# Gated attention block on one core: the last chunk's x loaded at once and bo\*gate added ahead, the denominators' test in one matmul behind the last y, routing in four stages, and the third last tile's matmuls split two, one and one

## The chip, the cores and the metric

The kernel runs on one core of a Trainium2 chip. The metric is the device time of one execution in microseconds (us). An interval or a ratio is always against the kernel before on the same chip.

## What is computed

The input x is 2 batches of 1024 tokens with 512 features, all in float32. Two branches read the same layernorm of x, and their product is added to x:

```python
xn = layernorm(x)
# attention, 32 heads of 16 features, causal
q, k, v = (xn @ W.T + b for W, b in ((Wq, bq), (Wk, bk), (Wv, bv)))
att = softmax(where(causal, q @ k.T / sqrt(16), -inf))
s = (att @ v) @ Wo.T + bo
# gate: a base projection and 8 experts of rank 16, of which the best two are used
probs = softmax(xn @ W_gate.T)
top_p, top_i = top_k(probs, 2)
route_w = one-hot(top_i) weighted by top_p / sum(top_p)
hw = einsum('bnd,erd->bner', xn, A) * route_w
g = silu(xn @ W_base.T + b_base + einsum('bner,eor->bno', hw, B))
out = x + s * g
```

## The kernel before

**Chunks, units and steps.** Each batch is two chunks of 512 tokens, (b, c), and each chunk four tiles of 128 tokens. A unit (b, oc, c) is the attention of eight heads (oc is one of four groups of 128 features) for one chunk's queries. The units are cut into a plan of 144 steps. A step's scores are sixteen or eight or more matmuls `s` (L913, transposed: keys on partitions), an Exp on ScalarE into `pt` (L922), a causal mask on VectorE where the step has a diagonal block (`masked`, L941), and matmuls `av` with the values (L957), where a column of ones beside the values gives the denominators of the softmax.

**Program order.** The program is written out by hand, with no scheduler behind it. Each step issues the scores of step n, the values of step n - 1, the masks of step n, and then `fill(n)`. Each engine takes its instructions in this order. A step's score tiles use all the PSUM that scores have, so the next `s` waits for `pt` of the step before; `av` waits for the masks.

**Filler tasks.** `fill` gives TensorE other work, so many matmuls that the rest of the work is spread evenly over the remaining steps. The tasks are generators, sorted by a due step: `qk_task` (pq, pk), `v_task` (pv), `route_task` (ph: the experts' first projection and the routing logits), `gate_task` (pb, and then g, sg and g\*sg), `out_task` (po, the output projection). A task yields its cost in TensorE time (`MM`) after each block of 128 rows of a contraction, which the profile shows as eight matmuls, or `WAIT` where it may go on in the next step at the earliest. Tasks without a TensorE cost (layernorm, routing, the test) are stepped at the end of `fill`, behind the posts of finished units in `later`.

**Routing.** `routed_task` (L409) takes the logits of a chunk: maximum, difference (L427), Exp on ScalarE (L428), then the sum, reciprocal and product of a softmax, the top two with ties to the lower index (`top`), their normalization, the product `hw` with the experts' first projection and a transpose `hsq` (L457, L464), a DMA to DRAM, and back as `hwT` one step later. It is cut in two stages by one `WAIT`. `gate_task` may start three steps after it ended.

**Posts of a unit.** When a unit ends, VectorE copies its two av tiles to oT and avs (L978, L980). A few steps later the denominators, spread over partitions by way of DRAM, are inverted on VectorE (rc, L543), avs is halved on GpSimd (L547) and merged on VectorE (L548: merge), and the inverse is brought back by DMA into avs and multiplied in (rb, L556 and L557).

**Last chunk.** The last unit's steps go tile by tile: its av is copied to avs per tile (L975), turned (`pt_o`, L571), divided on VectorE (L579, L580: olast), turned again (`pt_y`, ScalarE copy L617) and put through po. Tiles 0 and 1 are `whole_task`, with three VectorE operations per tile: po + bo, times g, plus x. Tile 2 (the title's third last tile) is a `whole_task` with `hold`, which runs from the last step's fill on, with its last two operations on GpSimd (L633, L634). Tile 3 is `most_task` (three of four blocks of po, ahead: its y, times g, plus x go into base) and `rest_task` (the last block). Each tile loads its own x (xr, L87). The last `fill` gives tile 2 `3 * MM`, three of its four blocks; the fourth follows the second `pt_o`.

**Test.** The kernel divides without the maximum of a softmax; all denominators must lie in a range, else a general kernel behind a branch computes everything again. `test_task` tests those of the units before the last (`first_fine`). In `rest_task`, `all_in_range` tests the last unit's (L676, L677), takes the minimum over columns (L685), multiplies the two (L686), counts partitions with one matmul `pn` (L688) and writes the count to `sound` (L689). All engines read `sound` at the end and branch.

## Time and profile before

| | |
|---|---|
| median of 3 runs | 635.23 us (635.17 to 635.51) |
| the profiled execution's own time | 635.22 us |
| its span | 632.30 us, so 2.92 outside the span |
| granted TensorE clock | 0.995 |
| TensorE busy | 619.9 us, 98% of the span |
| ScalarE, VectorE, GpSimd busy | 47%, 45%, 16% |
| pt, Exp on ScalarE (L922) | 288 of 1.02 us |
| mask on VectorE (L941) | 166 of 0.61 us |
| avs halved on GpSimd (L547) | 15 of 1.70 us |
| g\*sg on GpSimd in one place (L514, 577.38) | 1.27 us |

In lines of the timeline the first number is the start in microseconds from the start of the span and the second is the time; `x8` is the number of instructions in the group. In brackets stands the idle time of the engine ahead of the group and what ended it. A step of the plan is seen on TensorE as one group of s, one of av and the filler.

### The profile page before, as it was taken

What the parts mean: (1) busy time and instruction counts of PE and PEld (TensorE: products, weight loads), DVE (VectorE), ACT (ScalarE), POOL (GpSimd) and SP (SyncE); (2) the same over time, 40 slices, a digit from 0 to 9 for tenths busy, and PEclk for the clock granted to TensorE, in tenths of its full rate; (3) what the DMA queues carried; (4) which work ended last, traced back from release to release, by engine and by line L of the source; (5) the groups of instructions that cost most, each with busy time, mean ns of one, the idle gap of its engine ahead of it and who ended that gap; (6) DMA issues with size and microseconds to landing.
All of it is one profiled execution on the core that took longest, in us unless ns stands there. A gap on an engine that the chain in (4) does not pass through costs nothing.

```text
span 632.3 us, 15592 instructions
## 1 busy us (share of the span) xinstructions
PE 619.9 (98%) x6911; PEld 232.5 (37%) x6911; DVE 283.8 (45%) x584; ACT 298.0 (47%) x336; POOL 104.1 (16%) x128
## 2 busy tenths in 40 slices
PE   8999999999999999999999999999999999999993
PEld 8335322322334333332333322342233343245651
DVE  4454722322593627640545522326245636143543
ACT  2425344555555556554434544254445555535550
POOL 2101000010122003320351103300013200242301
PEclk9999999999999999999999999999999999999998
DMA  9903000030013040220110001200000001121012
GB/s 270 277 37 104 24 18 2 2 71 1 2 49 96 1 101 4 73 87 1 56 64 6 5 20 44 76 4 20 18 4 3 4 6 53 35 69 51 7 36 72
DMA packets 29515, 29.61 MB, mean 47 GB/s; under 512 B 6920, under 2 KB 19728, under 8 KB 29440
## 3 DMA queue, kind: packets, MB, share of 16 engines
q1 hardware_dynamic: 29424, 28.53, 15.2%
q8 instruction: 56, 0.92, 0.6%
q14 instruction: 19, 0.16, 0.1%
q10 hardware_dynamic: 16, 0.00, 0.0%
HBM read 19.65 MB, written 8.88 MB: 45 GB/s over the span
## 4 chain that ended last, share of the span: by engine, by line
PE 93%; DVE 4%; issue 1%; POOL 1%; ACT 1%; POOLq 0%; DVEq 0%
PE s L913 24%; PE av L957 22%; PE pb L197 10%; PE po L197 8%; PE pq L197 8%; PE pv L197 8%; PE pk L197 8%; PE ph L197 2%; PE warm L149 1%; PE pq_first L306 1%; ACT pt L922 0%; PE pk_first L306 0%; POOL rstd L215 0%; PE pt_x L295 0%; DVE ok L677 0%
## 5 line engine op out<-in xcount | busy, mean ns | idle before, releaser
L922 ACT ACTIVATE pt<-s 128x1024 f32<-128x1024 f32 x288 | 279.0, 1020 | 263.7 <-PE s L913 263.6
L913 PE MATMUL s<-qT,kT 32*128 32x512 f32 (+3 forms) x1824 | 168.9, 464 | 0.3 <-ACT pt L922 0.2
L941 DVE TENSOR_TENSOR pt<-pt,causal 128x256 f32<-128x256 f32 (+1 forms) x166 | 99.2, 612 | 143.0 <-ACT pt L922 143.0
L957 PE MATMUL av<-pt,v 128*32 128x512 f32 (+3 forms) x1824 | 155.7, 443 | 0.3 <-DVE oT L978 0.2
L913 PEld LDWEIGHTS s<-qT,kT 32*128 32x128 f32 x1824 | 74.1, 184 | 119.8 <-ACT pt L922 79.7
L957 PEld LDWEIGHTS av<-pt,v 128*32 128x32 f32 x1824 | 43.6, 109 | 90.3 <-issue 68.2
L197 PE MATMUL pb<-wb_sb,xnT 128*32 128x512 f32 x512 | 61.9, 592 | 0.0
L197 PE MATMUL po<-wo_sb,oT 128*32 128x512 f32 x512 | 60.3, 593 | 0.4 <-ACT oT L617 0.4
L197 PE MATMUL pv<-wv_sb,xnT 128*32 128x512 f32 x512 | 60.0, 592 | 0.0
L197 PE MATMUL pq<-xnT,wq_sb 128*32 128x512 f32 x480 | 57.6, 592 | 0.0
L197 PE MATMUL pk<-xnT,wk_sb 128*32 128x512 f32 x480 | 56.8, 592 | 0.0
L513 POOL TENSOR_SCALAR sg<-sg 128x512 f32<-128x512 f32 x16 | 10.8, 672 | 259.8 <-ACT sg L512 259.8
L363 DVE TENSOR_SCALAR qT<-pq,b_sb,half 128x512 f32<-128x512 f32 x30 | 22.9, 805 | 49.4 <-PE pq L197 49.4
L547 POOL TENSOR_SCALAR avs<-avs,half 128x512 f32<-128x512 f32 x15 | 25.5, 1701 | 109.9 <-DMA den<-avs 85.6
L609 POOL TENSOR_TENSOR y<-y,g 128x512 f32<-128x512 f32 x12 | 15.3, 1274 | 90.8 <-DVE y L608 90.8
L197 PEld LDWEIGHTS pv<-wv_sb,xnT 128*32 128x32 f32 x512 | 16.8, 110 | 33.1 <-issue 32.4
L401 DVE TENSOR_TENSOR v<-pv,bv_sb 128x512 f32<-128x512 f32 x16 | 11.0, 690 | 39.7 <-PE pv L197 39.7
L197 PEld LDWEIGHTS pb<-wb_sb,xnT 128*32 128x32 f32 x512 | 16.7, 110 | 30.6 <-issue 29.9
L197 PEld LDWEIGHTS po<-wo_sb,oT 128*32 128x32 f32 x512 | 16.3, 110 | 31.5 <-issue 29.9
L197 PEld LDWEIGHTS pk<-xnT,wk_sb 128*32 128x32 f32 x480 | 15.5, 110 | 32.9 <-issue 32.6
L197 PEld LDWEIGHTS pq<-xnT,wq_sb 128*32 128x32 f32 x480 | 15.9, 110 | 30.7 <-issue 30.2
L512 ACT ACTIVATE sg<-g 128x512 f32<-128x512 f32 x16 | 10.1, 630 | 27.4 <-DVE g L509 20.3
(99 smaller groups left out, 318.9 us busy)
## 6 DMA issues: line engine op xcount, KB each, us to landing
x<-in_x_dram SPq DMA_DIRECT2D x16, 256.0 KB
xr<-in_x_dram SPq DMA_DIRECT2D x16, 256.0 KB
out_dram<-y SPq DMA_DIRECT2D x16, 256.0 KB
scr<-sq SPq DMA_DIRECT2D x6, 512.0 KB
xnT<-scr SPq DMA_DIRECT2D x24, 128.0 KB
wq_sb<-in_wq_dram SPq DMA_DIRECT2D x4, 256.0 KB
wk_sb<-in_wk_dram SPq DMA_DIRECT2D x4, 256.0 KB
wv_sb<-in_wv_dram SPq DMA_DIRECT2D x1, 1024.0 KB
```

The lines of the kernel that those rows point to most:

```text
L149: nc.tensor.matmul(warm[:, n % 4 * P : n % 4 * P + P], lhsT=ident, rhs=ident, start=True, stop=True)
L197: nc.tensor.matmul(o[j : j + 32], lhsT=lhsT[:, j : j + 32] if len(lhsT.shape) == 2 else lhsT[:, j // 32], rhs=rhs, start=start, stop=stop,)
L363: nc.vector.tensor_scalar(qT[:, par], pq, bq_sb[:, oc : oc + 1], half[:, par : par + 1], ALU.add, ALU.mult)
L401: nc.vector.tensor_add(vh[:, :, 0:HD], pv.rearrange("p (h r) -> p h r", h=H), bv_sb.rearrange("p (h r) -> p h r", h=H),)
L512: nc.scalar.activation(sg, gt, AF.Tanh, scale=0.5)
L513: nc.gpsimd.tensor_scalar(sg, sg, 0.5, 0.5, ALU.mult, ALU.add)
L547: nc.gpsimd.tensor_scalar(avs, avs, half[:, 1:2], None, ALU.mult)
L609: nc.gpsimd.tensor_tensor(y, y, gs.pop((b, i)), ALU.mult)
L913: nc.tensor.matmul(ss[s // 2][:, s % 2, col : col + w], lhsT=kT[rows, kt % TT * P : kt % TT * P + P], rhs=qTs[b, oc, c][rows, par, q0 : q0 ...
L922: nc.scalar.activation(pt[:, 2 * pair : 2 * pair + 2], ss[pair], AF.Exp, scale=0.25)
L941: nc.vector.tensor_tensor(d, d, mask, ALU.mult)
L957: nc.tensor.matmul(avs_now[par][32 * s : 32 * s + 32, q0 : q0 + w], lhsT=vs[b, kt][:, h * VS - HD * par : h * VS - HD * par + HP], rhs=pt[ ...
```

## The change

There are four parts.

1. The x of the last chunk comes in one DMA into the chunk tile (`bases_task`, due nine steps before the end) instead of four. `whole_task` forms bo\*g and adds it to x on GpSimd ahead of its po, so that `finish_tile` has two operations on VectorE: po times g, plus base.
2. `last_in_range` writes the test of the last unit's denominators as 32 columns of a tile `fine`, whose first column is the earlier test. One matmul with ones sums all 33 columns over partitions, behind the last po; VectorE reduces and copies the sum to `sound` behind the last y. The branch compares with 33 x 128.
3. The routing drops the softmax's division (it cancels in the normalization of the top two) and is cut in four stages: to the difference; Exp and the first `top`; the rest up to the weights; hw, hsq and the DMA.
4. The last `fill` gives two blocks of tile 2's po; a third is issued behind the last av, and the fourth where it was, behind the second `pt_o`.

```diff
+NF = 1 + 4 * 2 * 4
...
-    with tc.If(n < P, preferred_fallthrough_block=False):
+    with tc.If(n < P * NF, preferred_fallthrough_block=False):
...
         nc.vector.tensor_tensor(pr, lg, over(mx), ALU.subtract)
+        yield WAIT
         nc.scalar.activation(pr, pr, AF.Exp)
-        z = each("z")
-        nc.vector.tensor_reduce(z, pr, AX.X, ALU.add)
-        nc.vector.reciprocal(z, z)
-        nc.vector.tensor_tensor(pr, pr, over(z), ALU.mult)
...
         nc.vector.tensor_tensor(r1, r1, over(m1), ALU.mult)
+        yield WAIT
         hw = sb.tile([P, TT, ER], F32, tag="hw", bufs=1, name="hw")
...
+    def bases_task(b, c):
+
+        xt = chunk_tile(b, c)
+        nc.sync.dma_start(
+            out=xt, in_=x[b, c * C : (c + 1) * C].rearrange("(t p) d -> p t d", p=P)
+        )
+        for t in range(TT):
+            bases[t] = xt[:, t]
+        yield 0.0
+
+    def finish_tile(b, c, t, po):
+        i = c * TT + t
+        y = sb.tile([P, D], F32, tag="tmp", name="y")
+        nc.vector.tensor_tensor(y, po, gs.pop((b, i)), ALU.mult)
+        nc.vector.tensor_tensor(y, y, bases[t], ALU.add)
+        nc.sync.dma_start(out=out[b, i * P : (i + 1) * P, :], in_=y)
+
     def whole_task(b, c, t, hold=0):
...
-        while not turned or normalized(b, c) < KC - 1 or now[0] < hold:
+        while not turned or normalized(b, c) < KC - 1:
             yield WAIT
-        xt = load_x(b, i)
+        y, g = sb.tile([P, D], F32, tag="tmp", name="y"), gs[b, c * TT + t]
+        nc.gpsimd.tensor_tensor(y, bo_sb, g, ALU.mult)
+        nc.gpsimd.tensor_tensor(bases[t], bases[t], y, ALU.add)
+        while now[0] < hold:
+            yield WAIT
         po = mm_tile("po")
         for _ in project_out(po, b, c, t, 0, KC):
             yield MM
-        y = sb.tile([P, D], F32, tag="tmp", name="y")
-        nc.vector.tensor_add(y, po, bo_sb)
-        eng = nc.gpsimd if hold else nc.vector
-        eng.tensor_tensor(y, y, gs.pop((b, i)), ALU.mult)
-        eng.tensor_tensor(y, y, xt, ALU.add)
-        nc.sync.dma_start(out=out[b, i * P : (i + 1) * P, :], in_=y)
+        finish_tile(b, c, t, po)
         yield MM
...
     def rest_task(b, c, t):
...
+        last_in_range()
         yield lambda: turn_last(b, c, t, turned), TR
...
-        all_in_range()
-        y = sb.tile([P, D], F32, tag="tmp", name="y")
-        nc.vector.tensor_tensor(y, po, gs.pop((b, i)), ALU.mult)
-        nc.vector.tensor_tensor(y, y, bases[i], ALU.add)
-        nc.sync.dma_start(out=out[b, i * P : (i + 1) * P, :], in_=y)
+        pn = mm_tile("pn")[0:1, 0:NF]
+        nc.tensor.matmul(pn, lhsT=ones, rhs=fine, start=True, stop=True)
+        finish_tile(b, c, t, po)
+        count = small.tile([1, 1], F32, tag="count", bufs=1, name="count")
+        nc.vector.tensor_reduce(count, pn, AX.X, ALU.add)
+        nc.vector.tensor_copy(sound, count)
         yield MM
...
+    def last_in_range():
+        in_range(
+            fine[:, 1:NF], rc_last.rearrange("p a t s -> p (a t s)"), 1.0 / Z_HIGH, 1.0 / Z_LOW
+        )
...
+                Task(len(plan) - 9, bases_task(b, c), 0.0, after=before, takes={"x": 1})
...
         if n == len(plan) - 1:
-            even = 3 * MM
+            even = 2 * MM
...
     values(last, pts.pop(last))
+    third = next(x for x in tasks if x.begun)
+    third.step()
     turn_late()
```

## The prediction

> **What bounds the kernel now.** I read first the busy shares and the chain that ended last on the page.

> ```profile
> PE 619.9 (98%) x6911; PEld 232.5 (37%) x6911; DVE 283.8 (45%) x584; ACT 298.0 (47%) x336; POOL 104.1 (16%) x128
> PE 93%; DVE 4%; issue 1%; POOL 1%; ACT 1%; POOLq 0%; DVEq 0%
> ```

> TensorE's matmuls are the time. The changed program gives TensorE the same matmuls, but for the small one of the test, so only its stalls and the tail can move. A modelled busy time hides stalls, so the second view is the timeline of TensorE, where a step of the plan lasts from its first s to the next. With sixteen filler matmuls beside 4096 columns each of s and av, undisturbed steps last 3.78 to 3.81 us.

> ```profile
> 253.92 1.15 PE L913 MATMUL s<-qT,kT 32*128 32x256 f32 x16
> 257.71 1.14 PE L913 MATMUL s<-qT,kT 32*128 32x512 f32 x8
> 262.25 1.57 PE L913 MATMUL s<-qT,kT 32*128 32x512 f32 x8
> 435.55 2.05 PE L913 MATMUL s<-qT,kT 32*128 32x384 f32 x16 [0.20 <-ACT pt L922]
> 440.24 1.14 PE L913 MATMUL s<-qT,kT 32*128 32x512 f32 x8
> ```

> 253.92 to 257.71 is a whole step; 435.55 to 440.24 is 4.69, a stall of 0.89; 257.71 to 262.25 is 4.54, one of 0.76. Third, the timelines of the other engines say what each stall waited for.

> ```profile
> 434.13 0.19 DVE L427 TENSOR_TENSOR pr<-hl,mx 128x32 f32<-128x32 f32 x1
> ...
> 434.36 0.23 ACT L428 ACTIVATE pr<-pr 128x32 f32<-128x32 f32 x1 [3.46 <-DVE pr L427]
> ...
> 439.33 0.69 DVE L457 TENSOR_TENSOR hw<-hl,key 128x512 f32<-128x512 f32 x1
> ```

> The routing's Exp stands on ScalarE ahead of the next pt, whose s was done at 432.6, and waits for VectorE; then a row of small VectorE operations, with hw and hsq (0.71, from 440.06) at its end, stands ahead of masks that an av needs.

> **Routing in four stages.** Three small operations go (0.22 us each by their starts, 434.62 to 435.28). The Exp moves to the step after pr, so that ScalarE never waits, and hw and hsq (1.40 us) to a step of their own. The TensorE steps around the four routings exceed the whole step by: chunk (0,0) 0.69 and 0.31; (0,1) 0.32; (1,0) 0.26, 0.89 and 0.67; (1,1) 0.33. I take all of these as removed, 3.47, less 0.1 in (1,1), where the stage of eleven small operations (11 x 0.22 = 2.4) starts after kT at about 528.8 and so ends near 531.2, close ahead of masks that av needs by 532.2. Gain 3.4; bounds 1.0 (only what the Exp's wait and three operations cost) to 3.5. Step 124's stall of 0.85 stays: step 123 has no filler in either order, and its s waits for pt.

> **What the stages push.** hwT comes two steps later. In chunks (0,0) and (1,0) the order on TensorE is unchanged. In (1,1) po work is put ahead, and the gates land in steps without a merge beyond the one of before. In (0,1) the planner puts pv first, and g of tiles 5 and 7 finish in the same fills as rc and merge (steps 57 and 62), ahead of them on VectorE, and their sg and g*sg ahead of avs on GpSimd. One place of before has this very order:

> ```profile
> 575.19 0.68 DVE L509 TENSOR_TENSOR g<-pb,bb_sb 128x512 f32<-128x512 f32 x1
> 580.24 0.75 DVE L548 SCALAR_TENSOR_TENSOR oT<-oT,half,avs 128x512 f32<-128x512 f32 x1 [4.10 <-POOL avs L547]
> ...
> 576.68 0.62 POOL L513 TENSOR_SCALAR sg<-sg 128x512 f32<-128x512 f32 x1 [6.44 <-ACT sg L512]
> 577.38 1.27 POOL L514 TENSOR_TENSOR g<-g,sg 128x512 f32<-128x512 f32 x1
> 578.64 1.56 POOL L547 TENSOR_SCALAR avs<-avs,half 128x512 f32<-128x512 f32 x1
> ```

> Merge starts 5.05 us after g. There it costs nothing, since the next step has no masks; behind merge at step 57 stand four normalizations and the masks that av(58) waits for:

> ```profile
> 255.71 0.75 DVE L548 SCALAR_TENSOR_TENSOR oT<-oT,half,avs 128x512 f32<-128x512 f32 x1 [1.28 <-POOL avs L547]
> 256.38 1.91 DVE L222 TENSOR_SCALAR x<-x,mv,rstd 128x512 f32<-128x512 f32 x4
> 258.21 1.28 DVE L941 TENSOR_TENSOR pt<-pt,causal 128x512 f32<-128x512 f32 x2
> ```

> From merge's start to the masks' end is 3.78 us. g can start at 254.09, so merge at 259.14 instead of 255.71: av(58) and the next s come 3.43 later, of which 0.43 is won back, since g(6) no longer puts its sg ahead of pt in the step behind (its stall of before). Net 3.0. At step 62 g starts near 274.15, merge near 279.2, and the masks end about 280.4 to 280.7; av(63) began at 278.90. Cost 1.5. Sum 4.5; bounds 0 (the gates finish otherwise than their order says) and 5.0.

> **x and bo*gate early.** Four loads of x become one DMA of 1 MB at step 133. SP issues it behind back<-rc (576.16) and ahead of avs<-back, which waits for merge until 581.01; rb reads that at 588.84. Cost nothing by this cover of some 7 us; without it up to the excess. bo*g and base+= are two GpSimd operations (1.27 each) for tiles 0 to 2 as for the last one, run ahead; VectorE does two operations per tile instead of three (0.69 less), and tile 2 none on GpSimd at the end. Against it: a VectorE operation with two SBUF inputs waits for a running GpSimd one (L677 took 1.28 on 32 columns under GpSimd's L633, but 0.66 on 480 columns at 590.65), and tile 1's pair runs near the masks of step 140. Tile 2's pair waits for its buffer until tile 0's output has landed (SP's last output took 3.49 us; issued near 607.2, so 610.7), runs to about 613.2, and may hold the masks of step 142 for half a microsecond, ahead of an av that begins at 614.84. I take 0.0 for all this, since each av there has some 0.7 us of slack behind its masks; bounds 0 and 1.3.

> [...]

> **Test and third last tile: the tail.**

> ```profile
> 620.17 0.33 PE L571 MATMUL pt_o<-ident,avs 128*128 128x128 f32 x1 [0.41 <-DVE avs L975]
> 625.11 0.19 PE L688 MATMUL pn<-ones,fine 128*1 128x1 f32 x2 [1.93 <-DVE fine L686]
> ...
> 622.38 1.28 DVE L677 SCALAR_TENSOR_TENSOR ok<-rc_last,ok 128x32 f32<-128x32 f32 x1
> 623.91 1.05 DVE L686 TENSOR_TENSOR fine<-fine,first_fine 128x1 f32<-128x1 f32 x1
> 625.41 0.67 DVE L667 TENSOR_TENSOR y<-po,g 128x512 f32<-128x512 f32 x1
> 626.12 0.69 DVE L668 TENSOR_TENSOR y<-y,xr 128x512 f32<-128x512 f32 x1
> ...
> 626.84 0.34 SPq L669 DMA_DIRECT2D out_dram<-y  x1
> ```

> Before, the last y waited from 623.19 (po's end) to 625.41 behind the test, which ran under tile 2's GpSimd operations. Now one part of po (0.86) moves behind av(143) and covers the copy of avs, so the 0.41 goes: first pt_o 617.56, av 617.82, the moved po to 619.55, second pt_o 619.76, last part of po 620.02, pt_y 621.02 (was 621.43), last po 621.71 to 622.78. The two remaining test operations run on VectorE about 622.5 to 623.0 with no GpSimd beside them; then y 622.95 and 623.65, end 624.34. That was 626.81, so the last DMA goes 2.47 earlier. But every engine reads sound only after reduce and copy (0.18 + 0.15 and their starts), at about 624.75; VectorE's read was 626.13 and its queue ended 4.66 later. By the DMA the span ends 5.46 after its issue (632.30 - 626.84), 624.37 + 5.46 = 629.8; by VectorE's queue 624.75 + 4.66 = 629.4, with 0.75 to 1.5 after it 630.2 to 630.9. I take 630.2: gain 2.1, bounds 1.4 to 2.5.

> **Sum** against the profiled execution's own time (span 632.30 + 2.92 outside = 635.22; median of the runs 635.23): -3.4 + 4.5 - 2.1 = -1.0, so 634.2. Its own range is 632.5 to 635.8: a third of each term's way to its bounds, added.

> **Rivals.**
> *The late gates cost nothing.* Then -5.5: 629.7. For it: GpSimd is busy 16% only, and the place is priced by one instance. Against: the order of the queues is fixed, and both masks are read by the next av. Where only one of the two stalls bites, 631 to 633.
> *Slower: routing's stalls are not lifted.* As many VectorE operations but three remain ahead of masks in the following steps; if av still waits for them, routing gives 1.0, and -1.0 + 4.5 - 2.1 = +1.4, 636.6. It decides as soon as routing gives under 1.1 (4.5 - 2.1 - 1.3). For it: stage three stands ahead of masks at step 123. Against: at steps 11 and 101 no masks follow.
> *The tail does not move*, because all queues now read sound behind the last y: 634.2 + 2.1 = 636.3. Against: 624.75 is still 1.4 before VectorE's read of before.

> **How the numbers follow.** 0.2% (1.27 us) is about what a measurement of this kernel can tell from no change. As forecast: 0.60, split 0.24 faster, 0.31 same, 0.05 slower (the bound below, 633.96, lies just under the forecast). Late gates free or half free: 0.20, faster. Routing not lifted: 0.14, of it 0.11 slower, 0.03 same. Tail unmoved: 0.06, slower 0.04, same 0.02. Sums: faster 0.44, same 0.36, slower 0.20. The range reaches from 630.6 (inside the first rival) to 636.9 (past the slower two), leaving out about one in ten on each side.

> **What would show it.** Right: the steps at 70.5, 435.6 and 440.2 shrink to 3.8; the step after masks(58) grows from 4.54 to about 8, behind POOL avs and merge, and that of av(63) to 5.3; last y's end to end of span 5.5 to 6.5. Wrong: merge at step 57 close behind rc; masks(99 to 101) still late; or a last y later than 625.

## The result: no change that can be told, and the profile after

| | before | changed |
|---|---|---|
| median | 635.27 us (634.73 to 635.77, 12 runs) | 635.62 us (634.64 to 636.88, 12 runs) |
| ratio | | 1.0006 (95% interval 0.9997 to 1.0015) |
| the profiled execution | 635.22, span 632.3 | 635.92, span 634.2 |

The forecast was 634.2 with a range from 630.6 to 636.9; the time lies in the range, 1.4 above the forecast, and in the middle class.

The two spans may not be subtracted. The warm-up matmuls at the start took 5.42 us in the profile of before and 6.47 in that after, and between 5.33 and 6.73 over the profiles of this study; and the profile of before has 2.92 us outside its span, where later runs of the same kernel have about 1.86, with a median span of 633.4. So the parts are compared by steps, from the first s of a step to the next. The end has a spread of its own: from the end of the last y to the end of the span it took 5.49 us in the profile of before, and 5.83, 5.91 and 6.20 in three other profiles of kernels that end with the old test.

These lines of the page after answer to those of before; the third is of its groups of instructions.

```profile
PE 619.5 (98%) x6911; PEld 231.9 (37%) x6911; DVE 281.5 (44%) x570; ACT 298.0 (47%) x336; POOL 110.1 (17%) x132
PE 91%; issue 4%; DVE 2%; POOL 2%; ACT 1%; POOLq 0%; DVEq 0%
L967 PE MATMUL av<-pt,v 128*32 128x512 f32 (+3 forms) x1824 | 155.4, 444 | 4.9 <-DVE pt L951 4.9
```

TensorE now waits 4.9 us for masks, a line that was 0.3 before and named no mask. The timeline of TensorE after shows where:

```profile
253.63 1.15 PE L923 MATMUL s<-qT,kT 32*128 32x256 f32 x16
257.42 1.14 PE L923 MATMUL s<-qT,kT 32*128 32x512 f32 x8
262.07 1.86 PE L967 MATMUL av<-pt,v 128*32 128x256 f32 x14 [3.51 <-DVE pt L951]
264.15 3.00 PE L198 MATMUL pb<-wb_sb,xnT 128*32 128x512 f32 x14
267.07 1.14 PE L923 MATMUL s<-qT,kT 32*128 32x512 f32 x8
284.78 1.39 PE L967 MATMUL av<-pt,v 128*32 128x512 f32 x8 [1.42 <-DVE pt L951]
```

Step 59 lasts from 257.42 to 267.07, 9.65 instead of 4.54, and av waits 3.51 us of it. But behind the wait fourteen pb matmuls took 3.00 us, where the same fourteen took 1.89 in the profile before. The busy times by window, with the granted clock as the number ahead of the DMA share, say why:

```profile
258.50:262.00 3.50, 0.06 (x4) 0.00 (x0) 3.16 (x7) 1.94 (x2) 0.30 (x1) 1.00 0.02 5
263.00:266.00 3.00, 3.00 (x26) 1.05 (x20) 2.13 (x5) 0.00 (x0) 0.00 (x0) 0.50 0.41 167
267.00:271.00 4.00, 4.00 (x38) 1.14 (x40) 0.86 (x3) 2.02 (x3) 0.00 (x0) 1.00 0.47 129
```

After the wait the clock was at 0.50 for 3.41 us, from 262.96 to 266.37. What VectorE and GpSimd did meanwhile is what the forecast said: g, then merge behind GpSimd's three operations.

```profile
253.76 0.69 DVE L508 TENSOR_TENSOR g<-pb,bb_sb 128x512 f32<-128x512 f32 x1
258.84 0.75 DVE L547 SCALAR_TENSOR_TENSOR oT<-oT,half,avs 128x512 f32<-128x512 f32 x1 [4.12 <-POOL avs L546]
261.33 1.28 DVE L951 TENSOR_TENSOR pt<-pt,causal 128x512 f32<-128x512 f32 x2
...
255.97 1.28 POOL L513 TENSOR_TENSOR g<-g,sg 128x512 f32<-128x512 f32 x1
257.24 1.57 POOL L546 TENSOR_SCALAR avs<-avs,half 128x512 f32<-128x512 f32 x1
```

And the tail, by VectorE's and TensorE's timelines after: the test's two operations take 0.17 and 0.19, the last y follows po at once, and the count comes behind it.

```profile
626.69 0.17 DVE L688 TENSOR_SCALAR fine<-rc_last 128x32 f32<-128x32 f32 x1
626.90 0.19 DVE L689 SCALAR_TENSOR_TENSOR fine<-rc_last,fine 128x32 f32<-128x32 f32 x1
627.01 0.68 DVE L634 TENSOR_TENSOR y<-po,g 128x512 f32<-128x512 f32 x1
627.73 0.69 DVE L635 TENSOR_TENSOR y<-y,x 128x512 f32<-128x512 f32 x1
628.54 0.14 DVE L683 CAST sound<-count 1x1 int32<-1x1 f32 x1
...
625.84 1.06 PE L198 MATMUL po<-wo_sb,oT 128*32 128x512 f32 x8 [0.35 <-ACT oT L616]
```

Between the two profiles the steps changed so:

| part | change, us |
|---|---|
| start, up to the first s | +1.05 (differs from run to run) |
| steps 10, 11, 48, 99, 100, 101, 122 (routing) | -0.69 - 0.31 - 0.32 - 0.26 - 0.90 - 0.67 - 0.33 = -3.48 |
| steps 59, 60, 64 (late gates) | +5.11 - 0.43 + 1.81 = +6.49 |
| steps 123 to 134, order of po and gates | +0.18 |
| last s to the end of the span (18.57, now 16.22) | -2.35 |

Without the start that is +0.84; the medians differ by 0.35, and the interval of the ratio reaches from -0.2 to +1.0. The difference of 0.5 is inside the spread of the end.

### The profile page after: what moved, and what is told of

It reads as the page before. It is cut to its first block, busy times and chain, and to the rows that moved or that the text cites. A ratio compares the mean times of both kernels' runs of the same rounds, so it can differ in the third digit from the quotient of the medians.

```text
span 634.2 us, 15574 instructions
## 1 busy us (share of the span) xinstructions
PE 619.5 (98%) x6911; PEld 231.9 (37%) x6911; DVE 281.5 (44%) x570; ACT 298.0 (47%) x336; POOL 110.1 (17%) x132
## 4 chain that ended last, share of the span: by engine, by line
PE 91%; issue 4%; DVE 2%; POOL 2%; ACT 1%; POOLq 0%; DVEq 0%
PE s L923 23%; PE av L967 21%; PE pv L198 9%; PE po L198 9%; PE pb L198 8%; PE pk L198 8%; PE pq L198 8%; PE ph L198 2%; PE warm L150 1%; ACT pt L932 1%; POOL g L513 1%; PE pq_first L307 1%; POOL avs L546 0%; PE pk_first L307 0%; DVE st L212 0%
## 5 line engine op out<-in xcount | busy, mean ns | idle before, releaser
L923 PE MATMUL s<-qT,kT 32*128 32x512 f32 (+3 forms) x1824 | 166.7, 464 | 0.3 <-ACT pt L932 0.2
L951 DVE TENSOR_TENSOR pt<-pt,causal 128x256 f32<-128x256 f32 (+1 forms) x166 | 101.2, 623 | 137.4 <-ACT pt L932 137.3
L198 PE MATMUL pb<-wb_sb,xnT 128*32 128x512 f32 x512 | 63.4, 603 | 0.0
L512 POOL TENSOR_SCALAR sg<-sg 128x512 f32<-128x512 f32 x16 | 10.8, 673 | 249.8 <-ACT sg L511 249.8
L377 DVE TENSOR_SCALAR kT<-pk,b_sb 128x512 f32<-128x512 f32 x15 | 11.3, 750 | 31.2 <-PE pk L198 31.0
```

The lines of the kernel that those rows point to most:

```text
L198: nc.tensor.matmul(o[j : j + 32], lhsT=lhsT[:, j : j + 32] if len(lhsT.shape) == 2 else lhsT[:, j // 32], rhs=rhs, start=start, stop=stop,)
L377: nc.vector.tensor_scalar(kT, pk, bk_sb[:, oc : oc + 1], None, ALU.add)
L512: nc.gpsimd.tensor_scalar(sg, sg, 0.5, 0.5, ALU.mult, ALU.add)
L923: nc.tensor.matmul(ss[s // 2][:, s % 2, col : col + w], lhsT=kT[rows, kt % TT * P : kt % TT * P + P], rhs=qTs[b, oc, c][rows, par, q0 : q0 ...
L951: nc.vector.tensor_tensor(d, d, mask, ALU.mult)
```

## Experiments

Theory: the routing gains 3.5, the tail 2.3, and the gates that moved two steps give both back, through two waits for merge and through a halved clock behind the longer of them. Rivals: that only the waits cost; that the routing's stalls were something else; that the tail's gain is not real.

### The parts alone

The kernel before with only the hunks of `routed_task`:

```diff
+        yield WAIT
         nc.scalar.activation(pr, pr, AF.Exp)
-        z = each("z")
...
+        yield WAIT
         hw = sb.tile([P, TT, ER], F32, tag="hw", bufs=1, name="hw")
```

> The kernel before with the routing in four stages alone. Theory (late gates): the seven routing stalls go (-3.5 us, as between the two profiles), and the merge of steps 57 and 62 waits behind the gates' GpSimd work: steps 59 and 64 exceed a whole step by 5.9 and 1.8 instead of 0.8 and 0, with step 60 0.4 shorter, and 1.7 of the 5.9 is TensorE at half clock after its 3.5 us of waiting. Sum -3.5 + 5.1 - 0.4 + 1.8 + 0.2 = +3.2, 638.5. Rival 1 (only the waits cost, the slow matmuls come from another part of the change): +1.5, 636.8. Rival 2 (routing's stalls were not what the four stages removed): +5 or more.

Measured 638.05 against 635.16, ratio 1.0044 (1.0031 to 1.0058), +2.9. The seven routing stalls are gone, and steps 59 and 64 exceed a whole step by 5.77 and 1.80. The routing part alone makes the kernel slower, as the theory had it; rivals 1 and 2 are both off by more than a microsecond.

The changed kernel with the routing of before (the same hunks undone):

> The changed kernel with the routing of before (division and two stages), so that the early x, the test behind the last y and the two-one-one split are alone. Theory: from the last s to the end of the span 16.25 us instead of 18.57, -2.3, 632.9, with steps 59 and 64 as in the kernel before. Rival (part of the end lies outside the span, where the two profiles differ by 1.2 us: 2.92 before, 1.72 after): -3.5, 631.8, if that belongs to the tail; -1.1, 634.2, if the tail's gain is given back there.

Measured 632.73 against 635.16, ratio 0.9959 (0.9945 to 0.9973), -2.4. Steps 59 and 64 are as before (0.76 and 0). The two parts add up to +0.5; the whole measured +0.35. So nothing is lost between them, and the tail's gain is real. The spans of these runs are 3.1 shorter than before (medians 630.2 and 633.3), and the time outside the span is 0.5 longer (2.33 and 1.86); why it is longer stays open.

### The gates' place or the queue on GpSimd

```diff
+        def halve():
+            nc.gpsimd.tensor_scalar(avs, avs, half[:, 1:2], None, ALU.mult)
...
         def merge():
...
-            nc.gpsimd.tensor_scalar(avs, avs, half[:, 1:2], None, ALU.mult)
...
+        ahead.append((n + 3 + wait, halve))
         later.append((n + 3 + wait, merge))
...
+        for x in [x for x in ahead if x[0] <= n]:
+            ahead.remove(x)
+            x[1]()
```

The last three lines stand at the start of `fill`.

> The changed kernel, with the halving of avs on GpSimd issued at the start of the fill in which merge stands, ahead of that fill's sg and g*sg; nothing else moved. Theory (merge waits behind the gate's GpSimd work): merge follows rc within about 1 us at steps 57 and 62, step 59 exceeds by 0.8 at most, step 64 by 0, no half clock, so -5.9 + 0.8 - 1.8 = -6.9 against the changed kernel, 628.7. Rival (the gates' place itself costs, through VectorE's g and ScalarE's sg ahead of pt): less than -4, above 631.6.

Measured 629.91 against 635.16, ratio 0.9916 (0.9902 to 0.9929); against the changed kernel's 635.62 that is -5.7, and the two ratios give the same. Merge follows rc and step 64 has no stall, so the theory's wait is shown: one instruction ahead of two on GpSimd's queue. 1.2 less came than expected. VectorE's timeline of this run, then GpSimd's:

```profile
254.71 0.75 DVE L549 SCALAR_TENSOR_TENSOR oT<-oT,half,avs 128x512 f32<-128x512 f32 x1 [0.49 <-POOL avs L541]
255.38 3.17 DVE L223 TENSOR_SCALAR x<-x,mv,rstd 128x512 f32<-128x512 f32 x4
258.47 1.28 DVE L958 TENSOR_TENSOR pt<-pt,causal 128x512 f32<-128x512 f32 x2
...
254.76 1.18 POOL L512 TENSOR_SCALAR sg<-sg 128x512 f32<-128x512 f32 x1
256.02 1.33 POOL L513 TENSOR_TENSOR g<-g,sg 128x512 f32<-128x512 f32 x1
```

The four normalizations take 3.17 us instead of 1.91, beside GpSimd's two operations, and the masks stand behind them: step 59 exceeds by 1.80, not 0.8. In the changed kernel GpSimd was done at 258.81, and the normalizations began at 259.51.

```diff
+        if (b, c) == (1, 1):
+            yield WAIT
         normalize(tiles[0:2], *s0)
```

> The kernel with the halving first, and the four normalizations of the last layernorm one step later, behind the masks of step 58 instead of ahead of them. In the run with the halving first they took 3.17 us instead of 1.91, beside GpSimd's sg and g*sg, and step 59 exceeded a whole step by 1.8. Theory (they waited for GpSimd, and the masks for them): step 59 exceeds by 0, -1.8 against the halving first, 628.1. Rival (the masks wait for GpSimd themselves, wherever the normalizations stand): step 59 still exceeds by 1 or more.

Measured 628.19 against 635.44, ratio 0.9890 (0.9874 to 0.9907). VectorE's timeline:

```profile
255.98 2.53 DVE L960 TENSOR_TENSOR pt<-pt,causal 128x512 f32<-128x512 f32 x2 [0.17 <-ACT pt L941]
258.43 1.90 DVE L223 TENSOR_SCALAR x<-x,mv,rstd 128x512 f32<-128x512 f32 x4
```

The normalizations are at 1.90 again. The masks took their place beside GpSimd, 2.53 instead of 1.28, but they come earlier, and step 59 exceeds a whole step by only 0.21. Both theories had a part: each of these VectorE operations took longer beside GpSimd (3.17 instead of 1.91, 2.53 instead of 1.28), and what counts is which one an av waits for. What holds them up, no run shows.

### The slow matmuls behind the wait

```diff
+        if n == 58:
+            busy = mm_tile("busy")
+            for m in range(13):
+                nc.tensor.matmul(
+                    busy[:, m % 4 * P : m % 4 * P + P], lhsT=ident, rhs=ident, start=True, stop=True
+                )
```

> The changed kernel with 13 idle matmuls of 128x128 more (result not read) on TensorE between s and av of step 59, where it waits 3.5 us for the masks; they take about 3 us and end before the masks. Theory (the clock is halved because TensorE was idle): the wait stays, but av and pb behind it run at full clock, step 59 lasts 8.0 instead of 9.65, -1.7 against the changed kernel, 633.9. Rival (the matmuls were slow for another reason, as transfers or VectorE's and ScalarE's use of the memories): step 59 unchanged, 635.6, or longer by what the added matmuls outlast the wait.

Measured 633.48 against the changed kernel's 635.62: -2.1 (the two ratios to before give the same), ratio to before 0.9973 (0.9963 to 0.9982). TensorE's timeline, and then the window behind the wait:

```profile
258.76 3.17 PE L960 MATMUL busy<-ident 128*128 128x128 f32 x26
262.35 1.44 PE L973 MATMUL av<-pt,v 128*32 128x256 f32 x14 [0.42 <-DVE pt L951]
263.83 1.89 PE L198 MATMUL pb<-wb_sb,xnT 128*32 128x512 f32 x14
```

```profile
264.00:267.00 3.00, 3.00 (x29) 0.72 (x22) 1.40 (x3) 0.17 (x1) 0.00 (x0) 1.00 0.46 180
```

Step 59 lasts 7.96: the masks come as late as before, and the fourteen pb take 1.89 at full clock. Work that nobody reads made the kernel faster; the rival of transfers or memories is out, since the DMA share in that window is as high (0.46, and 0.41 at half clock in the changed kernel).

The same with 3 and 7 matmuls asks how long a wait it takes.

> The changed kernel with 3 added matmuls of 128x128 in the wait of step 59 instead of 13: about 0.7 us of work, so that TensorE still waits some 2.8 us. If the halved clock needs nearly the whole 3.5 us of idle time: the clock stays full and step 59 lasts 8.0, as with 13. If a shorter wait is enough: step 59 lasts about 9.6 as without them.

> The same with 7 added matmuls, about 1.7 us of work, which leaves a wait of about 1.8 us. Step 64 of the changed kernel waited 1.42 at full clock, so the theory expects full clock and a step 59 of 8.0; the rival (a share of idle time in a window, not one long wait, decides) about 9.6 in some profiles.

With 3 the wait was 2.64 us and the clock was halved; step 59 lasted 9.51, and the median was 635.06. With 7 the wait was 1.76, the profile's step 59 lasted 7.97 at full clock, and the median was 633.93. The window from 263 to 264 with 3, and then with 7:

```profile
263.00:264.00 1.00, 1.00 (x14) 0.47 (x10) 1.00 (x3) 0.00 (x0) 0.00 (x0) 0.50 0.00 0
```

```profile
263.00:264.00 1.00, 1.00 (x16) 0.35 (x10) 1.00 (x4) 0.00 (x0) 0.00 (x0) 1.00 0.00 0
```

But with 7 three of the ten runs took 635.8 to 635.9 and the other seven 633.0 to 634.6, so that about two microseconds seem to come back in some runs. No profile of such a run was taken, so this reading is inferred; their mean granted clock, 0.995, is also that of one of the seven and doesn't settle it. The expectation that a wait under 3.5 us leaves the clock alone is wrong at 2.64.

### Steps without filler

```diff
+        if 119 <= n <= 124:
+            even = (2, 1, 1, 1, 1, 2)[n - 119] * MM
```

> As the run with the normalizations later, and in addition the eight blocks of pq and pk that fill steps 119 to 122 spread over 119 to 124 (two, one, one, one, one, two). Theory (steps 123 and 124 wait for pt because they have no filler): their excesses of 0.24 and 0.9 go, -1.1, 627.0. Rival (with one block a step the other steps come to wait for pt as well): -0.3 at most.

Measured 628.20, no change from 628.19. The rival holds: with one block of filler, steps 121 and 123 wait for pt as well (they exceed by 0.29 and 0.42, and 124 by 0.32, together 1.03, where 123 to 125 had 1.32).

### The tail's parts and the division

> The kernel before with the two-one-one split alone. Theory (the last y waits for the test, which follows tile 2's y): pt_o's wait of 0.41 goes, and everything behind it, test and last y, moves by that: -0.4, 634.8. Rival (tile 2's GpSimd operations decide the end): 0.

The kernel before with `even = 2 * MM` and the two lines behind the last `values`: 634.90 against 635.29, ratio 0.9991 (0.9982 to 1.0001). The wait of 0.41 is gone and the last y ends 0.49 earlier after the last s; the time agrees with the expected -0.4 but is not clear of zero.

> The kernel before with the new test alone (its matmul behind the last po, the sum read behind the last y). Tile 2's two GpSimd operations stay at the end. Theory: last po still ends at 623.19; the y that reads PSUM follows, but the one with two SBUF inputs waits for GpSimd's second operation until 624.95 and ends near 625.7 instead of 626.81: -1.1, and the reads of sound come behind it: between -1.1 and 0, best -0.7, 634.5. Rival (no wait for GpSimd): y ends at 624.8, -1.7 or more.

The kernel before with `last_in_range`, `pn` behind the last po and the sum behind the last y: 635.92 against 635.29, ratio 1.0006 (0.9996 to 1.0015). A miss. VectorE's timeline shows the expected wait for GpSimd, whose two operations ran from 623.47 to 624.74 and from 624.82 to 626.08; in the changed kernel, without them, the same two VectorE operations took 0.19 and 0.69:

```profile
623.51 1.28 DVE L681 SCALAR_TENSOR_TENSOR fine<-rc_last,fine 128x32 f32<-128x32 f32 x1
625.42 1.21 DVE L671 TENSOR_TENSOR y<-y,xr 128x512 f32<-128x512 f32 x1
```

The last y ends 1.3 earlier after the last s, as expected, but the span ends 1.0 later after it. From the end of the last y to the end of the span it took 7.82 us, where the other four profiles with the old GpSimd operations at the end took 5.49 to 6.20. In the trace VectorE's last instruction came 1.8 us behind those of the other engines; a transfer of the instruction queue falls in that time. Why, stays open.

> The kernel before with the early x and bo*gate alone; the test stays ahead of the last y. Theory (the test was slow because GpSimd ran beside it): its four operations take 0.2 each instead of 0.18, 1.28, 0.18 and 1.05, so the last y ends near 625.0 instead of 626.81: -1.9, 633.3. Rival (the test's cost was its chain through TensorE): -0.5 at most.

The kernel before with `bases_task`, the early bo\*gate and `finish_tile`, and the old test: 633.99 against 635.44, ratio 0.9976 (0.9967 to 0.9986), -1.45. The test's four operations take 0.17, 0.19, 0.19 and 0.16, as expected; the last y ends 1.2 earlier after the last s, not 1.9, because tile 2's last operation is now on VectorE ahead of the test. The rival is out by this. The parts of the tail, -0.4, +0.6 and -1.45, don't add up to -2.4. That the test behind the last y pays only when GpSimd is done is not shown: in the test alone the last y did come earlier, and what was lost was lost behind it, in the end that stays unexplained.

> The kernel before, its routing still in two stages, without the softmax's sum, reciprocal and product (they cancel). Theory: the waits for the Exp stay, and the masks behind the first stage come 0.66 earlier, so 0.7 to 1.5 us of the 3.5 go: best -1.0, 634.2. Rival (the stages alone lifted the stalls): 0. Beside it: the time outside the span was 2.9 and 2.7 with the old routing and 1.7 in four profiles with the new; if it is the three operations, it is 1.7 here as well and the time a further 1.0 lower.

The kernel before without the three operations, in two stages: 634.03 against 635.44, ratio 0.9978 (0.9968 to 0.9988), -1.4. Steps 10, 11 and 101 shrink by 0.31, 0.31 and 0.39, together 1.0. So about 1.0 of the routing's 3.5 is the division and the rest the stages. The time outside the span was 1.82 in this profile and about 1.85 in the later runs of the kernel before, so the three operations don't set it. It was longer with the early x and the routing of before, 2.0 to 2.7 in the runs of the tail alone and 2.0 to 2.2 in those of the early x alone, and 1.4 to 1.5 in those of the test alone; no run says why.

## Why the prediction was right where it was, and the step that failed

**Routing.** -3.4 forecast, -3.48 in the profile. Each stall went whole. The rival that they are not lifted is out by the first run.

**x and bo\*gate early.** 0 forecast, 0 in steps 138 to 143: a mask at 609.60 took 1.11 instead of 0.42 beside GpSimd, but steps 140 and 142 last 3.23 to 3.24 us, as before. So the slack behind the masks covered it.

**Tail.** -2.1 forecast, -2.35 in the profile and -2.4 in the runs of the tail alone. The last y ends 10.47 us after the last s instead of 13.08; 5.75 us from its end to the span's end, inside the 5.5 to 6.5 that were named. The rival that the reads of sound hold it back is out.

**Late gates: the term that was mis-sized.** Place, order and wait were right: merge came 5.08 us after g (5.05 forecast). But the term was 4.5, with bounds of 0 and 5.0, and measured 6.49. Step 59 was to last about 8 and lasted 9.65; with the wait filled it lasted 7.96. The step that failed is the one that has av(58) and the next s come later by the length of the wait and no more, the price of a wait at its own length: TensorE's 3.5 us without work were followed by 3.41 us at half clock, 1.69 us more. The other 0.3 is step 64 (5.60 instead of 5.3); its av took 1.39 instead of 1.07 while VectorE was still at the masks (284.30 to 286.26).

**Sum.** -3.48 + 6.49 + 0.18 - 2.35 = +0.84 by the profiles, +0.35 by the medians, forecast -1.0; with the clock in the sum it would have been +0.7. That the time fell in the range and in the middle class in spite of a term 2.0 too small is in part luck: the range took in both, and the class that was given the highest chance was faster, 0.44 against 0.36.

The run that beats both kernels keeps all four parts, takes avs ahead of sg on GpSimd and the normalizations behind the masks: 628.19 us, 1.1% under the kernel before.

## What to carry to other kernels

When a planner moves work by a step, list for each engine's queue what now stands ahead of what, above all where two chains share a slow engine: one instruction moved ahead of two was worth 5.7 us here. A long wait of TensorE can cost more than its length: behind 3.5 us here the matmuls ran at half clock and lost 1.7 us more, and behind 1.76 us, in its profile, they didn't. Price such a wait with the clock, or fill it. And parts of a change can have opposite signs: measured together they were nothing, apart +2.9 and -2.4.

## What the runs showed of the hardware that was not expected

Four fp32 normalizations (one SBUF input, scalars from SBUF) took 3.17 us beside GpSimd and 1.91 without, so these operations, with a single SBUF tensor, were held up as well as the two-input masks (2.53 instead of 1.28).
